# All transfers of the softmax sums in the order in which they become ready, in GpSimd's and SyncE's queues

## The chip, the cores and the metric

The kernel runs on one core of a Trainium2 chip. The metric is the device time of one execution in microseconds. Five engines work side by side, each through its own list of instructions in a fixed order: TensorE (PE), VectorE (DVE), ScalarE (ACT), GpSimd (POOL) and SyncE (SP). The last two mostly issue DMA transfers here. An instruction whose semaphores are not yet set holds everything behind it on the same engine.

## The reference

Two layers on x of shape (16, 256, 32, 32). Each adds to x a self-attention of its group-normalised input, with 4 heads of 64 channels over the 1024 positions:

```python
q, k, v = (einsum('oc,bcn->bon', W, xf) + b for each of q, k, v)     # 4 heads of d = 64
sim  = einsum('bhdi,bhdj->bhij', q, k)
qpos = einsum('hdi,bhdj->bhij', (rel_h + rel_w), q)
attn = softmax(sim + qpos, axis=-1)
out  = einsum('bhdn,bhmn->bhdm', v, attn)
x = x + out
```

The softmax needs, for each of 1024 query positions of each head, the sum of 1024 exponentials. How these sums are brought together is what the change touches.

## The kernel before

The schedule is written out by hand; nothing reorders it. A *unit* is one image in one layer, 32 in all. A unit has four *blocks*: two pairs of heads (`pr`) by two halves of the query positions (`half`), 128 blocks n = 0 to 127. An *even* block has half 0, an *odd* one half 1; the two blocks of one pair of heads are A (even) and B (odd) below. In tile names the numbers are unit, pair and half: `acc_21_0_1` belongs to unit 21, pair 0, half 1, which is block 85.

In a block TensorE makes eight score tiles (L539) on banks that DVE has seeded with the position term (L503), ACT takes the exponential of each into a tile `p` (L552), TensorE multiplies by the values (L592) and ACT copies the output out (L653, once a block, at its end). The projections of a later unit are woven in between.

The eight `p` of a block, each 128 key positions by 2 heads by 512 queries, are added up in these steps, which the page names by line:

- L557, DVE: `first` = p0 + p1, and `acc` = p3 + p4; L572, DVE: p5, p6, p7 are added to `acc`. The addition of p7 stands in the next block: at its start if that block is even, near its middle if it is odd.
- L568, POOL: a DMA of 512 KB that adds p2 to `first`. It is issued with `add_up(blk, 1)`.
- L609, POOL (`add_first`): 512 KB, adds `first` to `acc`; it needs the addition of p7.
- L614, POOL (`fold`): 256 KB, adds the upper 64 partitions of `acc` to the lower 64.
- L628, SP (`stack_up`): two of 64 KB, copy 32 partitions of `acc` into rows of `stack`, which A and B share.
- L633, POOL (`fold_again`): two of 64 KB, add the other 32 partitions of `acc` to the same rows. With them `acc` is free.
- L638, POOL (`fold_stack`): five transfers that halve the stack's 128 rows to 4, called D (64 rows onto 64, 128 KB), R (32), R/2 (16), R/4 (8) and R/8 (4 rows, 8 KB) after their argument. Each needs the one before it.
- L646, SP (`spread_sums`): four of 2 KB, bring the four rows into `den_all`.
- L688, DVE, and L690, L695, SP (`reciprocals`): 1/sum, sent to DRAM and from there back to all partitions in two copies of 256 KB. In an odd block this stands right behind the addition of A's p7.

Each POOL and SP transfer waits, at its place in the queue, until the ones that it depends on have landed. `first` and `acc` come from one pool of four buffers. Loads of x (L113) and stores of the output (L712) are in SP's queue too.

Of the kernel before, what the change touches and what calls it, by code (L numbers as in the profile page):

```python
# [56 lines left out]
def fast_path(ctx, tc, sh, x, layers, out, W, den_all, good, flag):  # L57
# [27 lines left out]
    B, C, H, N, CC, NT, NH, D, GT = (  # L85
        sh.B, sh.C, sh.H, sh.N, sh.CC, sh.NT, sh.NH, sh.D, sh.GT
    )
# [520 lines left out]
    def add_first(blk):  # L608
        nc.gpsimd.dma_start(accs[blk], firsts.pop(blk), accum_op=ALU.add)  # L609
# [25 lines left out]
    def fold_stack(u, pr, rows_):  # L635

        stack = stacks[u, pr]
        nc.gpsimd.dma_start(stack[:rows_], stack[rows_ : 2 * rows_], accum_op=ALU.add)  # L638

    def spread_sums(u, pr):  # L640

        stack, n = stacks.pop((u, pr)), index[u, pr, 0]
        for x in range(2):
            for h, hs in enumerate(QUARTERS):
                g = 2 * x + h
                nc.sync.dma_start(den_all[hs, n + x, :], stack[g : g + 1, :])  # L646
# [141 lines left out]
    def block(n):  # L788
# [11 lines left out]
        summed = blocks[n - 4][:2] if even and n > 3 else None  # L800
# [10 lines left out]
        if folded and even:  # L811
            add_first(previous)
        if even:
# [17 lines left out]
            if summed:  # L831
                fold_stack(*summed, R // 8)
                spread_sums(*summed)
# [38 lines left out]
            if folded:  # L872
                fold_again(previous)
            norms(u, b, 2)
# [26 lines left out]
            if summed and n == FOLDED:  # L901
                reciprocals(*summed)
# [5 lines left out]
        else:  # L908
# [11 lines left out]
            if stacked:  # L920
                fold_stack(*stacked, D)
            if stacked:
                fold_stack(*stacked, R)
            if not plain:
                k_half(w, pr, 1, qk)
# [15 lines left out]
            if folded:  # L941
                add_first(previous)
            if n > 4 and not last:
                reciprocals(*blocks[n - 5][:2])
# [20 lines left out]
            scores(after, 0)  # L965
            if folded:
                fold(previous)
                stack_up(previous)
            if stacked:
                fold_stack(*stacked, R // 2)  # L970
            if folded:
                fold_again(previous)
# [5 lines left out]
            if stacked:  # L978
                fold_stack(*stacked, R // 4)
                if last:  # L980
                    fold_stack(*stacked, R // 8)
                    spread_sums(*stacked)
# [528 lines left out]
```

## Time and profile before

| | us |
|---|---|
| median of 3 runs | 2529.62 |
| lowest, highest | 2519.19, 2544.5 |
| profiled execution | 2537.24 |
| its span, first to last instruction | 2535.5 |
| busy: PE, DVE, ACT, POOL | 2482.9, 2362.9, 2057.3, 796.4 |

The granted TensorE clock of the profiled execution was 0.995 of full speed. Busy times overlap, since the engines run side by side; POOL's busy time is that of issuing its transfers, most of its time it waits. In a row of the timeline stand the start, the duration, the engine, the line and the tiles (written <- read), and in brackets how long the engine was idle before it and what ended that. A transfer's own time is not its row's duration but the time to its landing, which the DMA view gives as a median for each kind.

### The profile page before, as it was taken

The numbers are of one execution on the slowest core, as the hardware profiler recorded it, in microseconds if no ns is written. First come the engines' busy times: TensorE is split into PE (matmuls) and PEld (weight loads), VectorE is DVE, ScalarE is ACT, GpSimd is POOL, SyncE is SP. The second block draws the span as 40 slices with busy tenths as digits, with TensorE's granted clock in tenths as the row PEclk, the third lists the DMA queues.
The fourth block names the chain that finished last, engine by engine and source line by source line (L and its number), as shares of the span: only waits on it lengthen the run. The fifth ranks groups of instructions, "written<-read, shape, count | busy, mean of one in ns | idle before, by whom it ended". The sixth has DMA issues, their size and how long they took to land. (4 is left out here: it accounts for less than half of the span.)

```text
span 2535.5 us, 86433 instructions
## 1 busy us (share of the span) xinstructions
PE 2482.9 (98%) x36976; PEld 1766.0 (70%) x36976; DVE 2362.9 (93%) x2816; ACT 2057.3 (81%) x4296; POOL 796.4 (31%) x937
## 2 busy tenths in 40 slices
PE   7999999999999999999999999999999999999997
PEld 4777777777767767777676777767776676677764
DVE  7899999999999999899999999999999999899998
ACT  5888888888888888788887888888878888788764
POOL 0223333333333333333332333333333333333230
PEclk9999999999999999999999999999999999999999
DMA  2555556566556555665565556565665555556552
GB/s 86 111 96 104 109 111 112 110 129 137 111 109 141 112 105 111 124 120 113 116 115 118 114 111 121 108 132 115 120 126 119 114 104 112 109 95 122 113 112 73
DMA packets 137704, 286.64 MB, mean 113 GB/s; under 512 B 55896, under 2 KB 57432, under 8 KB 137312
## 3 DMA queue, kind: packets, MB, share of 16 engines
q0 software_dynamic: 71568, 195.12, 44.6%
q1 hardware_dynamic: 65744, 85.90, 11.9%
q8 instruction: 293, 4.80, 0.8%
q14 instruction: 99, 0.81, 0.1%
HBM read 51.78 MB, written 17.30 MB: 27 GB/s over the span
## 5 line engine op out<-in xcount | busy, mean ns | idle before, releaser
L503 DVE TENSOR_TENSOR banks<-abt 128x1024 f32<-128x1024 f32 x1207 | 1239.6, 1060 | 100.5 <-ACT p L552 58.6
L552 ACT ACTIVATE p<-banks,shift 128x1024 f32<-128x1024 f32 x898 | 980.1, 1114 | 278.1 <-PE banks L539 162.4
L539 PE MATMUL banks<-q,k 64*64 64x512 f32 x8192 | 1114.5, 593 | 9.6 <-DVE banks L503 9.6
L592 PE MATMUL banks<-p,v 64*64 64x256 f32 x16384 | 963.6, 377 | 0.0
L592 PEld LDWEIGHTS banks<-p,v 64*64 64x64 f32 x16384 | 783.1, 133 | 182.6 <-issue 38.9
L539 PEld LDWEIGHTS banks<-q,k 64*64 64x64 f32 x8192 | 470.9, 133 | 305.6 <-issue 121.4
L633 POOL DMA_DIRECT2D stack<-acc x248 | 210.8, 964 | 842.2 <-DMA stack<-acc 688.1
L572 DVE TENSOR_TENSOR acc<-acc,p 128x1024 f32<-128x1024 f32 x372 | 454.0, 1220 | 4.2
L638 POOL DMA_DIRECT2D stack<-stack x310 | 309.9, 1000 | 386.4 <-DMA stack<-stack 225.1
L401 PE MATMUL banks<-t,form 64*64 64x512 f32 x1984 | 405.2, 589 | 0.0
L437 PE MATMUL banks<-Wv,xn 64*64 64x256 f32 x4096 | 302.1, 378 | 0.7 <-ACT v L462 0.7
L437 PEld LDWEIGHTS banks<-Wv,xn 64*64 64x64 f32 x4096 | 229.8, 133 | 43.6 <-PEq L193 17.5
L401 PE MATMUL banks<-xn,form 64*64 64x512 f32 x992 | 259.3, 589 | 0.0
L288 ACT ACTIVATE xn<-x,nshift,rstd 128x128 f32<-128x128 f32 x496 | 211.7, 500 | 29.4 <-DVE nshift L281 29.4
L568 POOL DMA_DIRECT2D first<-p x124 | 220.6, 1779 | 36.7 <-ACT p L552 33.3
L614 POOL DMA_DIRECT2D acc<-acc x124 | 103.1, 831 | 386.0 <-DMA acc<-first 373.4
L213 ACT ACTIVATE junk<-x,neg 128x128 f32<-128x128 f32 x505 | 199.9, 404 | 0.0
L609 POOL DMA_DIRECT2D acc<-first x124 | 185.5, 1496 | 36.6 <-DVE acc L572 33.3
L401 PEld LDWEIGHTS banks<-t,form 64*64 64x64 f32 x1984 | 137.7, 133 | 71.1 <-issue 33.9
L557 DVE TENSOR_TENSOR acc<-p,p 128x1024 f32<-128x1024 f32 x128 | 156.2, 1221 | 32.0 <-issue 18.2
L550 ACT ACTIVATE p<-banks,shift 128x512 f32<-128x512 f32 x252 | 159.5, 684 | 23.1 <-PE banks L539 17.3
L557 DVE TENSOR_TENSOR first<-p,p 128x1024 f32<-128x1024 f32 x124 | 150.9, 1217 | 2.4 <-DMA acc<-first 2.1
(102 smaller groups left out, 1761.9 us busy)
## 6 DMA issues: line engine op xcount, KB each, us to landing
first<-p POOLq DMA_DIRECT2D x124, 512.0 KB, 8.0
acc<-first POOLq DMA_DIRECT2D x124, 512.0 KB, 5.6
rden<-rd SPq DMA_DIRECT2D x126, 256.0 KB, 4.4
acc<-acc POOLq DMA_DIRECT2D x124, 256.0 KB, 4.5
x<-in_x_dram SPq DMA_DIRECT2D x32, 512.0 KB, 3.8
stack<-acc SPq DMA_DIRECT2D x248, 64.0 KB, 2.1
stack<-acc POOLq DMA_DIRECT2D x248, 64.0 KB, 2.8
out_dram<-x SPq DMA_DIRECT2D x31, 512.0 KB, 2.9
```

What stands on the lines that cost most here:

```text
L288: nc.scalar.activation(grouped(xns[u], g), grouped(xt[units[u][0]], g), AF.Identity, bias=shift[:, g : g + 1], scale=rstd[:, g : g + 1],)
L401: yield nc.tensor.matmul(ps[c, a, :], f[rs, left[a], c0 : c0 + D], right[a][rs, :], start=(t == 0 and step == 1 and a == 1), stop=(t == 1) ...
L437: yield nc.tensor.matmul(pv[c, a, i, :], xns[u][rs, cc, j0 : j0 + D], W.wv[l][rs, cc, :], start=(t == 0 and cc == 0 and i == 0), stop=(t = ...
L503: nc.vector.tensor_tensor(ps[:, h].rearrange("p h (w y) -> p h w y", y=H), ab[:, h, :H].unsqueeze(2).to_broadcast(shape), ab[:, h, H + hal ...
L539: nc.tensor.matmul(ps[c, h, :], a[hs, j0 : j0 + D], b[hs, columns], start=bool(tag) and i == 0, stop=i == len(terms) - 1, skip_group_check ...
L552: nc.scalar.activation(p, ps, AF.Exp, bias=W.shift)
L557: nc.vector.tensor_tensor(t, probs[blk, a], probs[blk, b], ALU.add)
L568: nc.gpsimd.dma_start(firsts[blk], probs[blk, 2], accum_op=ALU.add)
L572: nc.vector.tensor_tensor(accs[blk], accs[blk], probs[blk, j], ALU.add)
L592: yield nc.tensor.matmul(po[c, a, :QUART], vts[u, j // 4][rs, j % 4, c0 : c0 + D], p[rs, h, a * QUART : (a + 1) * QUART], start=(fresh and ...
L633: nc.gpsimd.dma_start(at, acc[R:D, h, :], accum_op=ALU.add)
L638: nc.gpsimd.dma_start(stack[:rows_], stack[rows_ : 2 * rows_], accum_op=ALU.add)
```

## The change

The steps and their sizes stay. Their places in the block's code move: A's `fold_again` and D go into the even block after the pair, R/2, R/4, R/8 and the spreads into the odd block after it, `stack_up` of A behind the spreads.

```diff
--- before.py
+++ after.py
@@ -797,7 +797,6 @@
             return block_without_pieces(n, half)
 
         stacked = blocks[n - 3][:2] if not even and n > 2 else None
-        summed = blocks[n - 4][:2] if even and n > 3 else None
         before = blocks[n - 6][:2] if even and n > 5 else blocks[n - 5][:2] if last else None
         after, previous = blocks[n + 1], blocks[n - 1] if n > 0 else None
         two = u + 2 < NU
@@ -810,6 +809,8 @@
             add_up(previous, 7)
         if folded and even:
             add_first(previous)
+            if n > 1:
+                fold_again(blocks[n - 2])
         if even:
             qk = psum2(tz, f"qk_{w}_{pr}") if not plain else None
             first = None if plain else first_product(w, pr, qk)
@@ -828,9 +829,6 @@
                 after_first(w, pr, qk)
             scores(blk, 2)
             add_up(blk, 1)
-            if summed:
-                fold_stack(*summed, R // 8)
-                spread_sums(*summed)
             v(1)
             if folded:
                 fold(previous)
@@ -871,6 +869,8 @@
             seed(after, 0, ta)
             if folded:
                 fold_again(previous)
+                if n > 1:
+                    fold_stack(*blocks[n - 2][:2], D)
             norms(u, b, 2)
             values_of_p = attend(blk, po, fresh=False)
             values_of_p(0)
@@ -898,8 +898,8 @@
             scores(after, 1)
             seed(after, 2, ta)
             add_up(blk, 6)
-            if summed and n == FOLDED:
-                reciprocals(*summed)
+            if n == FOLDED:
+                reciprocals(*blocks[n - 4][:2])
             seed(after, 3, tb)
             norms(u, b, 4)
             values_of_p(1)
@@ -918,9 +918,8 @@
                 reduced(2, 1)
                 added(2)
             if stacked:
-                fold_stack(*stacked, D)
-            if stacked:
                 fold_stack(*stacked, R)
+                fold_stack(*stacked, R // 2)
             if not plain:
                 k_half(w, pr, 1, qk)
             norms(u, b, 0)
@@ -940,6 +939,8 @@
             add_up(previous, 7)
             if folded:
                 add_first(previous)
+            if stacked:
+                fold_stack(*stacked, R // 4)
             if n > 4 and not last:
                 reciprocals(*blocks[n - 5][:2])
             scores(blk, 6)
@@ -963,23 +964,19 @@
             if two:
                 mean_out = (norm_mean if b == 1 else norm_var)(u + 2, pm)
             scores(after, 0)
+            if stacked:
+                fold_stack(*stacked, R // 8)
             if folded:
                 fold(previous)
-                stack_up(previous)
-            if stacked:
-                fold_stack(*stacked, R // 2)
-            if folded:
-                fold_again(previous)
             if u + 3 < NU and units[u + 3][1] == 0 and u > 0 or n == 3:
                 load_x(units[u + 3][0], range(pr_, pr_ + 1) if u > 0 else range(CC))
             seed(after, 1, tx)
             if last:
                 finish(*before)
             if stacked:
-                fold_stack(*stacked, R // 4)
-                if last:
-                    fold_stack(*stacked, R // 8)
-                    spread_sums(*stacked)
+                spread_sums(*stacked)
+            if folded:
+                stack_up(previous)
             if two:
                 mean_out()
                 if b == 3:
```

The POOL queue of before, from the L609 of block 84 (unit 21, pair 0, half 0) on; `stack_20_1` is the stack of the pair before it:

```order
L609 DMA acc_21_0_0_20257<-first_21_0_0_20107 128x1024
L568 DMA first_21_0_1_20383<-p_21_0_1_2_20329 128x1024
L614 DMA acc_21_0_0_20257<-acc_21_0_0_20257 64x1024
L638 DMA stack_20_1_19997<-stack_20_1_19997 16x512
L633 DMA stack_21_0_20477<-acc_21_0_0_20257 32x512 x2
L638 DMA stack_20_1_19997<-stack_20_1_19997 8x512
L609 DMA acc_21_0_1_20426<-first_21_0_1_20383 128x1024
L568 DMA first_21_1_0_20580<-p_21_1_0_2_20578 128x1024
L638 DMA stack_20_1_19997<-stack_20_1_19997 4x512
L614 DMA acc_21_0_1_20426<-acc_21_0_1_20426 64x1024
L633 DMA stack_21_0_20477<-acc_21_0_1_20426 32x512 x2
L638 DMA stack_21_0_20477<-stack_21_0_20477 64x512
```

and now:

```order
L609 DMA acc_21_0_0_20258<-first_21_0_0_20112 128x1024
L638 DMA stack_20_1_20006<-stack_20_1_20006 8x512
L568 DMA first_21_0_1_20385<-p_21_0_1_2_20330 128x1024
L638 DMA stack_20_1_20006<-stack_20_1_20006 4x512
L614 DMA acc_21_0_0_20258<-acc_21_0_0_20258 64x1024
L609 DMA acc_21_0_1_20428<-first_21_0_1_20385 128x1024
L633 DMA stack_21_0_20487<-acc_21_0_0_20258 32x512 x2
L568 DMA first_21_1_0_20585<-p_21_1_0_2_20583 128x1024
L614 DMA acc_21_0_1_20428<-acc_21_0_1_20428 64x1024
L633 DMA stack_21_0_20487<-acc_21_0_1_20428 32x512 x2
L638 DMA stack_21_0_20487<-stack_21_0_20487 64x512
L638 DMA stack_21_0_20487<-stack_21_0_20487 32x512
```

B's L609 (`acc_21_0_1`) stood behind A's `fold_again` (L633) and stands ahead of it; R/2, R/4 and R/8 of the older stack stood behind L614, L633 and L568, and stand ahead of L609, L568 and L614; R/2 follows R at once.

SP's queue of before at the same place, from the reciprocals of unit 20, pair 0 on:

```order
L690 DMA rd_20_0_20371<-r8_20_0_20369 128x16
L695 DMA rden_20_0_20373<-rd_20_0_20371 64x1024 x2
L628 DMA stack_21_0_20477<-acc_21_0_0_20257 32x512 x2
L113 DMA x_13_20483<-in_x_dram 128x1024
L646 DMA den_all_58<-stack_20_1_19997 64x1x8 x4
L628 DMA stack_21_0_20477<-acc_21_0_1_20426 32x512 x2
L690 DMA rd_20_1_20834<-r8_20_1_20832 128x16
L695 DMA rden_20_1_20836<-rd_20_1_20834 64x1024 x2
```

and now:

```order
L690 DMA rd_20_0_20373<-r8_20_0_20371 128x16
L695 DMA rden_20_0_20375<-rd_20_0_20373 64x1024 x2
L113 DMA x_13_20480<-in_x_dram 128x1024
L646 DMA den_all_58<-stack_20_1_20006 64x1x8 x4
L628 DMA stack_21_0_20487<-acc_21_0_0_20258 32x512 x2
L628 DMA stack_21_0_20487<-acc_21_0_1_20428 32x512 x2
L690 DMA rd_20_1_20836<-r8_20_1_20834 128x16
L695 DMA rden_20_1_20838<-rd_20_1_20836 64x1024 x2
```

The spreads (L646) stood ahead of B's `stack_up` and stand ahead of A's.

The DVE's list keeps its order, but the pool gives out its four buffers in another rotation, since they are given back at other places. What the L557 of blocks 84 to 86 wait for, before (DMASW are semaphores of POOL's transfers, DMAHW of SP's):

```order
L557 TENSOR_TENSOR first_21_0_0_20107<-p_21_0_0_0_19994,p_21_0_0_1_20073 128x1024 [waits DMASW6_49,DMASW5_49]
L557 TENSOR_TENSOR acc_21_0_0_20257<-p_21_0_0_3_20139,p_21_0_0_4_20155 128x1024 [waits DMAHW2_49,DMASW7_49,DMAHW3_49,DMASW2_49,DMASW1_49]
L557 TENSOR_TENSOR first_21_0_1_20383<-p_21_0_1_0_20244,p_21_0_1_1_20264 128x1024 [waits DMASW6_49,DMASW4_49]
L557 TENSOR_TENSOR acc_21_0_1_20426<-p_21_0_1_3_20339,p_21_0_1_4_20347 128x1024 [waits DMAHW1_49,DMASW7_49,DMAHW2_49,DMASW1_49,DMASW0_49]
L557 TENSOR_TENSOR first_21_1_0_20580<-p_21_1_0_0_20474,p_21_1_0_1_20538 128x1024 [waits DMASW5_49,DMASW4_49]
```

and now:

```order
L557 TENSOR_TENSOR first_21_0_0_20112<-p_21_0_0_0_19996,p_21_0_0_1_20078 128x1024 [waits DMASW7_49,DMASW6_49]
L557 TENSOR_TENSOR acc_21_0_0_20258<-p_21_0_0_3_20139,p_21_0_0_4_20155 128x1024 [waits DMASW3_49,DMASW0_49]
L557 TENSOR_TENSOR first_21_0_1_20385<-p_21_0_1_0_20245,p_21_0_1_1_20265 128x1024 [waits DMAHW0_49,DMASW5_49,DMAHW7_49,DMASW4_49,DMASW2_49]
L557 TENSOR_TENSOR acc_21_0_1_20428<-p_21_0_1_3_20340,p_21_0_1_4_20348 128x1024 [waits DMAHW1_49,DMASW7_49,DMAHW2_49,DMASW1_49,DMASW0_49]
L557 TENSOR_TENSOR first_21_1_0_20585<-p_21_1_0_0_20476,p_21_1_0_1_20543 128x1024 [waits DMASW6_49,DMASW5_49]
```

An even `acc` waited for `stack_up` and `fold_again` of the A before it, and now waits for the L609 of the block before it, whose `first` held the buffer. An odd `first` waited for the L609 of two blocks before, and now waits for `stack_up` and `fold_again` of the A of the pair before. An even `first` (L609 of two blocks before) and an odd `acc` (`fold_again` of two blocks before) wait as they did.

## The prediction

> **What bounds the kernel now.** I read the page first, for who is busy, then equal stretches of work side by side, then who the VectorE waits for, then the two DMA queues in order of time.
>
> ```profile
> span 2535.5 us, 86433 instructions
> PE 2482.9 (98%) x36976; PEld 1766.0 (70%) x36976; DVE 2362.9 (93%) x2816; ACT 2057.3 (81%) x4296; POOL 796.4 (31%) x937
> ```
>
> By the page TensorE sets the time. But a unit of work (four blocks; the counts differ by records that are missing) does not always take equally long. The view of stretches, with PE, weight loads, DVE, ACT and POOL busy in that order, then the granted clock, shows two units:
>
> ```profile
> 190.70:267.20 76.50, 76.50 (x1160) 54.95 (x1154) 73.00 (x88) 64.79 (x140) 25.22 (x30) 1.00 0.55 103
> 1310.30:1389.90 79.60, 76.82 (x1156) 54.96 (x1152) 73.25 (x88) 64.81 (x138) 25.65 (x31) 1.00 0.58 114
> ```
>
> 76.50 us is the undisturbed unit, where PE never idles; the second took 3.1 us more at the same clock and the same DVE work. How much that comes to over the run follows from the first and last copy of an output (L653, once a block) of 30 whole units, blocks 4 to 123:
>
> ```profile
> 114.17 0.57 ACT L653 COPY od<-banks 128x512 f32<-128x512 f32 x1
> 2442.14 0.59 ACT L653 COPY od<-banks 128x512 f32<-128x512 f32 x1 [2.33 <-PE banks L592]
> ```
>
> 2442.1 - 114.2 = 2327.9 us; 30 x 76.50 = 2295.0. So **32.9 us** are lost. Who loses them is in the view of L557, the DVE additions that open a new buffer `first` or `acc`: before them the DVE sat idle until
>
> ```profile
>   issue: 18.2, 20
>   DMA stack<-acc: 13.2, 8
>   DMA acc<-first: 2.5, 3
> ```
>
> 33.9 us in 31 waits (the "issue" ones have no releaser in the records, but stand at the same place, before `acc`). The two sums agree to 1 us: the lost time is DVE waiting for a buffer that the GpSimd queue has not yet freed. DVE then seeds the score banks late and PE stands. The queue itself waits almost always, and for what is in the view of waits:
>
> ```profile
> POOL stack L633 <- DMA stack<-acc: 688.1, 105, 9.7
> POOL acc L614 <- DMA acc<-first: 373.4, 121, 6.2
> POOL acc L609 <- DVE acc L572: 33.3, 2, 30.5
> ```
>
> It waits for its own earlier transfers, and only twice in 124 blocks for the DVE to hand it a new sum (L609), both in the first blocks. So it never catches up: it runs at its own pace. That pace is in the row of L609 in the view of the tile `acc`:
>
> ```profile
> L609 POOL DMA_DIRECT2D acc<-first x124: 870/1205/1906, 65.4 to 2455.2; - x124
> ```
>
> (2455.2 - 65.4) / 123 x 2 = 38.86 us a pair of blocks, where the undisturbed pair is 76.50 / 2 = 38.25. 0.61 us too much over 60 pairs is 36 us, near the 32.9 lost. **The kernel is paced by a serial chain of transfers that is 1.6% slower than TensorE.**
>
> **One turn of the chain.** The queue in order of time, from the L609 of block 84 to that of block 86 (start, duration, what; in brackets the idle time before), and below it SyncE's part:
>
> ```profile
> 1696.64 1.20 POOL L609 DMA_DIRECT2D acc<-first  x1
> 1703.57 0.82 POOL L614 DMA_DIRECT2D acc<-acc  x1 [4.82 <-DMA acc<-first]
> 1710.22 1.69 POOL L633 DMA_DIRECT2D stack<-acc  x2 [5.03 <-DMA stack<-acc]
> 1711.82 1.87 POOL L609 DMA_DIRECT2D acc<-first  x1
> 1717.80 0.84 POOL L614 DMA_DIRECT2D acc<-acc  x1 [1.86 <-DMA acc<-first]
> 1726.87 1.71 POOL L633 DMA_DIRECT2D stack<-acc  x2 [8.23 <-DMA stack<-acc]
> 1730.63 0.82 POOL L638 DMA_DIRECT2D stack<-stack  x1 [2.05 <-DMA stack<-acc]
> 1734.94 0.78 POOL L638 DMA_DIRECT2D stack<-stack  x1 [3.49 <-DMA stack<-stack]
> 1735.45 1.20 POOL L609 DMA_DIRECT2D acc<-first  x1
> ```
>
> ```profile
> 1707.68 1.13 SPq L628 DMA_DIRECT2D stack<-acc  x2
> 1721.79 2.42 SPq L646 DMA_DIRECT2D den_all<-stack  x4
> 1724.32 1.17 SPq L628 DMA_DIRECT2D stack<-acc  x2
> ```
>
> Call the even block A and the odd one B. Link by link: add A's `first` 6.93, fold A until SyncE stacks it 4.11, stacking 2.54, second fold into the stack 1.60, add B's `first` 5.98, fold B 6.52 (2.5 of it SyncE's four spreads, which stand ahead of the stacking), stacking 2.55, until D (the 64-row fold of the stack) 3.76, until R (32 rows) 4.31, until the next L609 0.51: 38.81 us.
>
> **The change part by part.** No transfer is added or removed, and PE, DVE and ACT keep their order. Landing times from the DMA view:
>
> ```profile
> first<-p POOLq DMA_DIRECT2D x124, 512.0 KB, 8.0
> acc<-first POOLq DMA_DIRECT2D x124, 512.0 KB, 5.6
> stack<-acc POOLq DMA_DIRECT2D x248, 64.0 KB, 2.8
> stack<-stack POOLq DMA_DIRECT2D x62, 64.0 KB, 2.5
> stack<-stack POOLq DMA_DIRECT2D x62, 8.0 KB, 6.5
> ```
>
> (the 8 KB fold lands late because it stands behind the 512 KB of L568). For L609 with L568 about 2 us behind it, as the new order has it, there are rows of the first blocks, when the queue still kept up:
>
> ```profile
> 98.71 0.84 POOL L638 DMA_DIRECT2D stack<-stack  x1 [2.95 <-DMA stack<-acc]
> 101.66 0.79 POOL L638 DMA_DIRECT2D stack<-stack  x1 [2.11 <-DMA stack<-stack]
> 105.23 0.89 POOL L609 DMA_DIRECT2D acc<-first  x1 [2.78 <-DVE acc L572]
> 107.30 0.86 POOL L568 DMA_DIRECT2D first<-p  x1 [1.18 <-DVE first L557]
> 111.66 0.82 POOL L614 DMA_DIRECT2D acc<-acc  x1 [3.49 <-DMA acc<-first]
> ```
>
> The new turn, us from A's L609:
>
> - R/4 (8 rows) needs R/2, issued 0.5 earlier: 2.2. L568 behind it: 2.7. R/8 needs R/4: about 6. A's fold L614: 6.43 by the early rows and 0.5 for the issue of R/8: 6.9. B's L609 is next in the queue: 7.4 at the earliest. Now it no longer waits for A to be stacked; this is the wait that goes, some 6 us of the old turn.
> - On SyncE the spreads come ahead of A's stacking. R/8 lands behind L568, 2.7 + 8.0 = 10.7; four spreads 2.5: 13.2; stacking 2.55: A's second fold L633 at 15.8. L568 of the next block 16.9, B's fold 17.8 (B's L609, 5.6, landed by then).
> - B's fold lands behind that L568 (16.9 + 5.6, nothing large ahead of it) and its own 1.5 (half of the 3.0 by which L568 lands after an L609 issued 0.6 before it): 24.0. No spreads ahead of the stacking now, so 2.5 us go here: 24.1; L633 26.7; D after 3.76: 30.4; R after 2.95 as in the early rows (at that time SyncE's two 256 KB copies don't run beside it): 33.4; then R/2, which now waits for R, after 2.7: 36.1; L609 0.5: **36.6 us**, 2.2 less than the old turn and 1.6 less than the 38.25 that TensorE gives it.
>
> The Trainium skill (DMA: Bandwidth & Descriptors, Anatomy of one DMA) gives a GpSimd-issued transfer 2.0 us fixed plus bytes / 436e3, which speaks against small dependent folds in a row: each pays it. By it the landings of D and R in the path cost 2.3 + 2.15 = 4.45 us by estimate; the rows above give 2.95 + 2.7 = 5.65, so the turn would be 35.4 by the page. The measured landings decide, and the verdict would be the same.
>
> Both ends: 34.2 us if the L568 ahead of R/8 lands in 5.6 instead of 8.0, and 39.6 if R and R/2 each take the 4.31 that the quoted turn shows from D to R. I take 36.6, near the early rows: the 4.31 was taken while SyncE's two 256 KB copies (L695) ran, and those start only after a reciprocal that follows A's last addition, while R now goes some 5 us ahead of that addition.
>
> One cost stands in no row above: A's stacking is now issued while B's L609 may be in flight. What SyncE's small transfers can suffer is in the landings of the spreads (L646):
>
> ```profile
> DMA to landing us min/median/max: 1.7/1.8/3.7
> ```
>
> The slowest takes twice the usual time. The bounds for A's stacking are then: no delay, and held until B's L609 has landed. The same page (Queues, rings and completion order) says that a semaphore's increment lands only after every earlier write of that DMA engine, across its queues; by that rule it would be the upper bound. When B's L609 goes depends on the DVE:
>
> ```profile
> 1106.24 1.22 DVE L572 TENSOR_TENSOR acc<-acc,p 128x1024 f32<-128x1024 f32 x1
> 1117.33 2.48 DVE L572 TENSOR_TENSOR acc<-acc,p 128x1024 f32<-128x1024 f32 x2
> 1120.86 1.22 DVE L557 TENSOR_TENSOR first<-p,p 128x1024 f32<-128x1024 f32 x1
> 1132.06 1.22 DVE L557 TENSOR_TENSOR acc<-p,p 128x1024 f32<-128x1024 f32 x1
> ```
>
> A's sum is ready at 1107.5, B's at 1119.8, 12.3 later. So if the queue has caught up, B's L609 goes at 12.3, lands at 17.9, and A's L633 moves from 15.8 to at most 18.1: the turn then takes up to 38.9. But a queue that is late issues B's L609 sooner, down to 7.4, and the delay goes: its own pace is 36.6. It settles a few us behind the DVE and stays there.
>
> How late may it be? In the new order an even `acc` takes the buffer that B's L609 frees: 1119.8 + 5.6 = 1125.4 against a need at 1132.1, 6.7 to spare. An even `first` needs A's L609: 1107.5 + 6.4 against 1120.9, 7.0 to spare. Odd blocks take buffers that the second folds free; B's, the later one, has landed at 26.7 + 0.6 + 2.8 = 30.1, and the need comes after the next A's sum, at 38.25. So lateness under 6 us costs nothing, and 1.6 us a turn are made up.
>
> **Sum.** All waits of the 30 units go: 2537.24 (the profiled execution, 1.7 above its span) - 32.9 = 2504.3. I leave 0.7 us for a stray wait: **2505 us**. What is late next is nothing: the unit is at 76.50, which the first units show with PE busy throughout. The profiled execution stands 7.6 above the median 2529.62, which by this reading had some 25 us of the same waits; the floor is common, so the gain on the median is 25 us, 1.0%. About 1% is also what a measurement of this kernel can tell from no change.
>
> **The rivals.**
>
> - The queue stays a little too slow: one of R and R/2 meets SyncE's copies, a load of x or a store (+1.4), and A's stacking is held by 0.5 on the mean: 38.5. For it: 4.31 in the quoted turn. Against: R's new place. 0.25 x 60 = 15 us stay: 2520.
> - **Slower:** the folds that now stand in a row. In the old order R/2, R/4 and R/8 are issued beside other waits; in the new one L609 stands behind R and R/2 both. If each takes 4.31, the turn is 39.6, and 1.35 x 60 = 81 us come over the floor: 2585. It decides from 38.86 a turn on, the old pace. Against: 2.95 and 2.5 in the rows without copies beside them.
> - The change does not do what it says: the waits move from `acc` to `first` or to the reciprocal, whose sums come by the same chain, and the total stays: 2530. Against: 6.7 and 7.0 us to spare at the new places, and the spreads now come earlier.
>
> **How the numbers follow.** Forecast (2500 to 2511) 0.67; queue a little too slow (2511 to 2531) 0.18; slower (2531 to 2600) 0.09; unchanged (2525 to 2535) 0.06. Range 2499 to 2527: the forecast and most of the second case, 0.81. Faster by over 1% means under 2504.3, the floor itself and what the last blocks may add to it: 0.42. Slower by over 1%, above 2555: 0.06. Within: 0.52.
>
> **What would show it.** L609 waiting for DVE L572 in most blocks instead of twice; L557 idle under 3 us in all; units of 76.50 throughout; A's L633 15 to 18 us after its L609; R and R/2 about 2.7 us apart. I am wrong if L609 still never waits for the DVE, or if units of 76.50 show up while the total does not fall.

## The result and the profile after

The changed kernel is slower: 2660.7 us in the median (2651.31 to 2662.86), against 2531.45 us for the kernel before beside it (2519.19 to 2544.5). The ratio is 1.050, with an interval of 1.044 to 1.056. The forecast was 2505 us.

The page of the changed kernel, the span and the busy times:

```profile
span 2658.2 us, 86471 instructions
PE 2536.6 (95%) x36976; PEld 1758.5 (66%) x36976; DVE 2356.5 (89%) x2816; ACT 2056.2 (77%) x4296; POOL 792.6 (30%) x937
```

DVE, ACT and POOL do the same work as before, within 1%; PE's share fell from 98% to 95%, and DVE's from 93% to 89%. So there is more waiting, not more work. (TensorE ran the same 36976 instructions too; why its busy time is 54 us longer stays open.) What L557 waited for, where 33.9 us stood before:

```profile
  DMA acc<-first: 97.6, 48
  issue: 15.6, 15
  DMA stack<-stack: 7.2, 3
  DMA stack<-acc: 3.3, 2
```

123.7 us, and most of it at another place: an even `first`, whose buffer A's L609 frees. The view of waits has two more lines to read:

```profile
ACT p L552 <- DMA first<-p: 107.2, 40, 4.4
POOL acc L609 <- DVE acc L572: 46.1, 6, 30.5
```

The first is new (0.8 us before): ACT waits to write a `p` buffer that L568 has not yet read. The second is the sign that the prediction asked for, L609 waiting for DVE "in most blocks": it did so 6 times. So the sign of being wrong came, "if L609 still never waits for the DVE", but for 6 of 124 blocks. The queue is later than before. Its pace, from the row of L609 in the view of the tile `acc`:

```profile
L609 POOL DMA_DIRECT2D acc<-first x124: 870/902/1213, 65.6 to 2574.0; - x124
```

(2574.0 - 65.6) / 123 x 2 = 40.79 us a pair of blocks, where 36.6 were forecast, 38.86 stood before, and TensorE gives 38.25. The excess over TensorE, 2.54 x 61.5 = 156 us, is the loss: 2660 - 156 = 2504, the floor of the prediction. Two stretches show when it begins, the first a unit and the second 80 us of the later run (length, then PE, weight loads, DVE, ACT, POOL busy, the granted clock):

```profile
190.70:267.20 76.50, 76.50 (x1156) 54.95 (x1152) 72.98 (x88) 64.82 (x139) 24.04 (x29) 1.00 0.54 99
1500.00:1580.00 80.00, 77.43 (x1142) 54.30 (x1138) 71.84 (x87) 64.01 (x137) 23.85 (x29) 1.00 0.53 102
```

The first is undisturbed; in the later 80 us PE is busy for 77.43, at the same clock. From the first to the last copy of an output of the 30 whole units (L653), a unit takes 81.64 us here and 77.60 before.

**One turn of the changed chain.** The GpSimd queue from the L609 of block 108 to that of block 110, then SyncE's part:

```profile
2279.75 1.18 POOL L609 DMA_DIRECT2D acc<-first  x1
2281.77 0.81 POOL L638 DMA_DIRECT2D stack<-stack  x1 [0.85 <-DMA stack<-stack]
2282.30 1.21 POOL L568 DMA_DIRECT2D first<-p  x1
2285.44 0.81 POOL L638 DMA_DIRECT2D stack<-stack  x1 [1.94 <-DMA stack<-stack]
2285.97 1.16 POOL L614 DMA_DIRECT2D acc<-acc  x1
2288.61 0.90 POOL L609 DMA_DIRECT2D acc<-first  x1 [1.48 <-DVE banks L503]
2296.65 1.68 POOL L633 DMA_DIRECT2D stack<-acc  x2 [7.15 <-DMA stack<-acc]
2297.72 1.51 POOL L568 DMA_DIRECT2D first<-p  x1
2298.26 1.83 POOL L614 DMA_DIRECT2D acc<-acc  x1
2308.54 1.69 POOL L633 DMA_DIRECT2D stack<-acc  x2 [8.45 <-DMA stack<-acc]
2312.63 0.84 POOL L638 DMA_DIRECT2D stack<-stack  x1 [2.39 <-DMA stack<-acc]
2317.75 0.79 POOL L638 DMA_DIRECT2D stack<-stack  x1 [4.29 <-DMA stack<-stack]
2320.48 0.77 POOL L638 DMA_DIRECT2D stack<-stack  x1 [1.94 <-DMA stack<-stack]
2321.01 1.18 POOL L609 DMA_DIRECT2D acc<-first  x1
```

```profile
2289.74 3.21 SPq L646 DMA_DIRECT2D den_all<-stack  x4
2293.06 2.24 SPq L628 DMA_DIRECT2D stack<-acc  x2
```

```profile
2306.00 1.11 SPq L628 DMA_DIRECT2D stack<-acc  x2
2310.10 0.33 SPq L690 DMA_DIRECT2D rd<-r  x1
2312.37 1.11 SPq L695 DMA_DIRECT2D rden<-rd  x2
```

Three places cost more than forecast. B's fold is issued at 2298.26 and B's stacking at 2306.00, 7.74 us later, with the 512 KB of L568 issued 0.54 ahead of the fold. D is issued at 2312.63, 0.26 us after SyncE's copies of `rden` (L695), and R follows only after 5.12 us. R itself has no copy beside it, and R/2 follows after 2.73, as forecast. And A's stacking, at 2293.06, releases A's L633 after 3.59 us instead of 2.55, with B's L609 (2288.61) ahead of it. The row of B's L609 names L503 of DVE, but what it waited for is L568 (2282.30), which had landed 0.56 us before it; in all of the 51 turns below B's L609 goes 0.55 to 0.83 us after that landing.

That this is the rule shows in the mean over 51 turns (A is block 18 to 118), worked out from the issue times in the traces, us after A's L609. "Stack" is SyncE's L628; the three folds of the stack are those of this pair:

| kernel | L614 A | L609 B | stack A | L633 A | L614 B | stack B | L633 B | D | R | R/2 | next L609 |
|---|---|---|---|---|---|---|---|---|---|---|---|
| forecast | 6.9 | 7.4 | 13.2 | 15.8 | 17.8 | 24.1 | 26.7 | 30.4 | 33.4 | 36.1 | 36.6 |
| after | 7.05 | 9.19 | 12.89 | 16.60 | 18.36 | 25.44 | 28.07 | 32.54 | 36.65 | 40.45 | 41.03 |
| before | 6.08 | 14.89 | 10.41 | 13.19 | 20.89 | 26.99 | 29.73 | 34.10 | 38.28 | – | 38.86 |
| sum_first_alone | 6.27 | 9.59 | 10.70 | 15.35 | 20.76 | 26.68 | 29.52 | 33.77 | 37.65 | – | 38.23 |
| spreads_behind_a_stacking | 6.94 | 9.44 | 11.15 | 15.46 | 17.20 | 24.15 | 26.85 | 31.12 | 34.68 | 38.65 | 39.23 |
| fold_again_back | 7.17 | 15.90 | 11.95 | 14.71 | 21.73 | 26.31 | 29.00 | 33.47 | 37.94 | 41.33 | 41.91 |
| spreads_behind_b_stacking | 6.59 | 16.41 | 11.61 | 14.66 | 22.56 | 27.16 | 29.89 | 34.39 | 37.67 | – | 38.32 |
| r2_behind_l609 | 6.12 | 14.03 | 13.01 | 15.87 | 19.66 | 26.25 | 29.09 | 33.31 | 36.40 | 39.66 | 38.27 |
| b_fold_ahead_of_l568 | 7.29 | 9.74 | 13.67 | 17.05 | 18.21 | 22.77 | 26.82 | 30.90 | 34.25 | 37.96 | 38.54 |
| reciprocals_9us_later | 7.29 | 9.63 | 13.38 | 17.04 | 18.85 | 25.76 | 28.40 | 32.78 | 36.12 | 40.37 | 40.95 |
| copies_behind_a_stacking | 7.23 | 10.86 | 13.18 | 17.30 | 19.44 | 26.26 | 28.96 | 33.46 | 36.55 | 39.44 | 40.53 |

("–": R/2 stands in the next turn there. A turn near 38.25 is TensorE's pace, at which the queue has time left.)

Up to B's fold the forecast is met within 1 us, but for B's L609, and A's L633 leads straight to B's fold (1.76 us instead of 7.70). The error grows from there on.

### The profile page after: what moved, and what is told of

It is laid out like the page before. It is cut to its first block, busy times and chain, and to the rows that moved or that the text cites. A ratio compares the mean times of both kernels' runs of the same rounds, so it can differ in the third digit from the quotient of the medians.

```text
span 2658.2 us, 86471 instructions
## 1 busy us (share of the span) xinstructions
PE 2536.6 (95%) x36976; PEld 1758.5 (66%) x36976; DVE 2356.5 (89%) x2816; ACT 2056.2 (77%) x4296; POOL 792.6 (30%) x937
## 3 DMA queue, kind: packets, MB, share of 16 engines
HBM read 51.78 MB, written 17.30 MB: 26 GB/s over the span
## 4 chain that ended last, share of the span: by engine, by line
DMA 54%; issue 17%; PE 9%; POOL 9%; SPq 5%; DVE 5%; ACT 1%; POOLq 0%; DVEq 0%; ACTq 0%
DMA stack<-stack 19%; DMA acc<-acc 18%; DMA stack<-acc 15%; SPq L646 4%; POOL stack L638 4%; PE banks L539 4%; POOL stack L633 3%; PE banks L592 3%; DVE banks L503 2%; POOL acc L609 2%; SPq L628 1%; DMA first<-p 1%; PE banks L401 1%; PE banks L437 1%; DVE acc L565 1%
## 5 line engine op out<-in xcount | busy, mean ns | idle before, releaser
L503 DVE TENSOR_TENSOR banks<-abt 128x1024 f32<-128x1024 f32 x1207 | 1234.7, 1058 | 141.5 <-ACT p L552 101.5
L539 PE MATMUL banks<-q,k 64*64 64x512 f32 x8192 | 1133.5, 598 | 84.6 <-DVE banks L503 84.5
L592 PEld LDWEIGHTS banks<-p,v 64*64 64x64 f32 x16384 | 801.6, 133 | 162.3 <-issue 35.7
L539 PEld LDWEIGHTS banks<-q,k 64*64 64x64 f32 x8192 | 440.7, 133 | 462.7 <-DVE banks L503 306.1
L638 POOL DMA_DIRECT2D stack<-stack x310 | 250.1, 807 | 774.9 <-DMA stack<-stack 580.5
L633 POOL DMA_DIRECT2D stack<-acc x248 | 209.3, 954 | 891.2 <-DMA stack<-acc 792.7
L401 PE MATMUL banks<-t,form 64*64 64x512 f32 x1984 | 412.1, 591 | 0.0
L401 PE MATMUL banks<-xn,form 64*64 64x512 f32 x992 | 281.2, 593 | 0.0
L557 DVE TENSOR_TENSOR first<-p,p 128x1024 f32<-128x1024 f32 x124 | 151.1, 1218 | 102.9 <-DMA acc<-first 95.4
L401 PEld LDWEIGHTS banks<-t,form 64*64 64x64 f32 x1984 | 149.1, 133 | 79.1 <-issue 43.4
L614 POOL DMA_DIRECT2D acc<-acc x124 | 178.0, 1436 | 4.8 <-DMA acc<-first 3.3
L557 DVE TENSOR_TENSOR acc<-p,p 128x1024 f32<-128x1024 f32 x128 | 155.9, 1218 | 21.2 <-issue 15.6
L568 POOL DMA_DIRECT2D first<-p x124 | 163.4, 1318 | 36.3 <-ACT p L552 32.7
L550 ACT ACTIVATE p<-banks,shift 128x512 f32<-128x512 f32 x252 | 158.9, 682 | 17.5 <-PE banks L539 16.6
L609 POOL DMA_DIRECT2D acc<-first x124 | 127.7, 1030 | 107.3 <-DVE acc L572 46.1
```

Source lines behind the costliest of these rows:

```text
L401: yield nc.tensor.matmul(ps[c, a, :], f[rs, left[a], c0 : c0 + D], right[a][rs, :], start=(t == 0 and step == 1 and a == 1), stop=(t == 1) ...
L503: nc.vector.tensor_tensor(ps[:, h].rearrange("p h (w y) -> p h w y", y=H), ab[:, h, :H].unsqueeze(2).to_broadcast(shape), ab[:, h, H + hal ...
L539: nc.tensor.matmul(ps[c, h, :], a[hs, j0 : j0 + D], b[hs, columns], start=bool(tag) and i == 0, stop=i == len(terms) - 1, skip_group_check ...
L557: nc.vector.tensor_tensor(t, probs[blk, a], probs[blk, b], ALU.add)
L592: yield nc.tensor.matmul(po[c, a, :QUART], vts[u, j // 4][rs, j % 4, c0 : c0 + D], p[rs, h, a * QUART : (a + 1) * QUART], start=(fresh and ...
L633: nc.gpsimd.dma_start(at, acc[R:D, h, :], accum_op=ALU.add)
```

## The experiments

The ratios are to the kernel before, run beside each on the same chip. Its median there was 2525 to 2540 us, so a difference between two rows of this table is good to some 10 us.

| kernel | made from | median us | ratio, interval |
|---|---|---|---|
| spreads_behind_b_stacking | before | 2506.63 | 0.987, 0.983 to 0.990 |
| sum_first_alone | before | 2504.67 | 0.987, 0.982 to 0.992 |
| sum_first_and_spreads | before | 2504.92 | 0.991, 0.989 to 0.993 |
| fold_again_back | after | 2726.78 | 1.075, 1.070 to 1.079 |
| spreads_behind_a_stacking | after | 2552.01 | 1.005, 1.002 to 1.008 |
| b_fold_ahead_of_l568 | after | 2530.70 | 1.003, 1.001 to 1.005 |
| both_mends | after | 2503.66 | 0.987, 0.984 to 0.989 |
| r2_behind_l609 | spreads_behind_a_stacking | 2502.84 | 0.991, 0.988 to 0.993 |
| reciprocals_late | after | 2816.51 | 1.113, 1.109 to 1.117 |
| reciprocals_9us_later | after | 2669.96 | 1.053, 1.049 to 1.057 |
| copies_behind_a_stacking | after | 2645.23 | 1.047, 1.044 to 1.051 |

### Does the queue pace the kernel before? The spreads behind B's stacking

```diff
                 fold_stack(*summed, R // 8)
-                spread_sums(*summed)
             v(1)
...
                 stack_up(previous)
+            if summed:
+                spread_sums(*summed)
             scores(blk, 5)
```

> The kernel before with SyncE's four spreads (L646) moved from ahead of B's stacking (L628) to behind it; the GpSimd queue is not touched. If the serial chain of the queue paces the kernel before, as the prediction read it, the 2.5 us of the spreads leave the turn: 38.9 - 2.5 = 36.4 us, under TensorE's 38.25, and the time is that of the undisturbed units, 2500 to 2512 us, with VectorE's wait at L557 under 5 us in all. If something else paces it (the lost time is not this queue's), it stays at 2525 to 2540 us.

2506.63 us. The row of L609 and all that L557 waited for:

```profile
L609 POOL DMA_DIRECT2D acc<-first x124: 870/1200/1908, 65.8 to 2420.7; - x124
```

```profile
  ACT p L552: 0.3, 1
```

38.29 us a pair, and L557 no longer waits for any transfer. Four 2 KB transfers moved on SyncE took 1.3% off the time; PE, DVE, ACT and the GpSimd queue have the same instructions in the same order. The reading of the kernel before, a chain of transfers that is 0.6 us a pair too slow, is shown, and with it a floor near 2505.

### Which part of the change is to blame? Three undone or done alone

One part done alone, B's L609 ahead of A's `fold_again` (R/4, which stood behind it, moves too):

```diff
             add_first(previous)
+            if n > 1:
+                fold_again(blocks[n - 2])
+        if summed:
+            fold_stack(*summed, R // 4)
         if even:
...
-            if folded:
-                fold_again(previous)
...
             if stacked:
-                fold_stack(*stacked, R // 4)
                 if last:
+                    fold_stack(*stacked, R // 4)
                     fold_stack(*stacked, R // 8)
```

> The kernel before with one part of the change alone: B's L609 is issued ahead of A's fold_again (L633), and R/4 with it; R/2, R/8, the spreads and the stacking stay where they were. Theory ROW (the change lost its time where the folds R, R/2 and R/4 each wait for the landing of the one before it ahead of the next 512 KB transfer): those folds are not moved here, so nothing is lost; L609 of A at 38 to 39 us a turn, 2505 to 2535 us. Theory HOLD (B's L609, in flight early, holds A's stacking on SyncE until it has landed, and that is what made the changed kernel slow): the same hold is here, A's L633 moves from 13.2 to 15 or later, and the time is 2560 us or more.

The same move of `fold_again` undone in the changed kernel (R/4 stays):

```diff
             add_first(previous)
-            if n > 1:
-                fold_again(blocks[n - 2])
...
                 stack_up(previous)
+                fold_again(previous)
```

> The changed kernel with A's fold_again (L633) back ahead of B's L609, so that B's L609 cannot be in flight while A is stacked; R, R/2 and R/4 stay in a row ahead of L609 and L568, the spreads stay ahead of A's stacking. Theory HOLD: the cause is gone, A's stacking to L633 takes 2.55 us again, and the time falls to that of the kernel before, 2530 us, or below. Theory ROW: D, R and R/2 still cost 3.8 us more a turn than before, and B's fold is later by some 4 us as in the kernel before: a turn of 41 us or more, 2650 to 2800 us.

2504.67 and 2726.78 us. Both come out on ROW's side: the part alone reaches the floor, and without it the changed kernel gets worse. HOLD as the cause of the slowdown falls. That the folds in a row cost time is not shown by these two; it is tested below. The hold itself is real, and the table shows it: from A's stacking to A's L633 pass 2.8 us before, 2.8 in fold_again_back and 2.9 in r2_behind_l609, where B's L609 goes later than the stacking; where it goes earlier, they are 3.7 after, 4.3 in spreads_behind_a_stacking and 4.7 in sum_first_alone. It costs 1 to 2 us where the prediction expected it to vanish, but B's earlier fold is worth more.

The spreads put back behind A's stacking:

```diff
-            if stacked:
-                spread_sums(*stacked)
             if folded:
                 stack_up(previous)
+            if stacked:
+                spread_sums(*stacked)
```

> The changed kernel with SyncE's spreads (L646) put back behind A's stacking (L628); nothing else is moved. Theory SPREADS (A's stacking waits for the spreads, whose R/8 lands late): A's stacking goes at about 11 us instead of 12.9, A's L633 up to 1.6 us earlier, the turn 39.4 instead of 41.0 and the time about 2570 us. Theory HOLD: the stacking is issued earlier but lands no sooner, since B's L609 is in flight: within 0.5 us a turn, 2630 to 2665 us. Theory ROW says little of this part: at most the 1.6 us, and the time stays over 2560 us.

2552.01 us, a turn of 39.23: 1.80 less, a little more than SPREADS expected, since 1.14 us come at A's L633 and the later folds meet less as well. So the change took the spreads out of B's path and put them into A's. They are worth about 109 us, and yet the kernel stays slower than before by 0.5%: they are not the whole cause.

### R/2 ahead of L609

```diff
                 fold_stack(*stacked, R)
-                fold_stack(*stacked, R // 2)
...
             if stacked:
-                fold_stack(*stacked, R // 4)
+                fold_stack(*stacked, R // 2)
...
-            if stacked:
-                fold_stack(*stacked, R // 8)
             if folded:
                 fold(previous)
+            if stacked:
+                fold_stack(*stacked, R // 4)
+                fold_stack(*stacked, R // 8)
```

> The kernel spreads_behind_a_stacking (2552 us, a turn of 39.2) with R/2 moved from ahead of A's L609 to right behind it, and R/4 and R/8 from ahead of L568 and of A's fold (L614) to behind A's fold. Theory ROW: the wait of R/2 for R's landing, 3.97 us from R to R/2 in that kernel's mean turn, leaves the path, and R/4 and R/8 cost about 0.5 more ahead of B's L609: 39.2 - 3.4 = 35.8, under 38.25, so 2503 to 2515 us. Rival: R and R/2 only fill time in which the turn waits for something else (B's chain or VectorE): the turn stays near 39 and the time within 10 us of 2552.

2502.84 us, ROW's figure. D, R, L609 and R/2 of one turn:

```profile
2090.39 0.82 POOL L638 DMA_DIRECT2D stack<-stack  x1 [2.91 <-DMA stack<-acc]
2093.38 0.79 POOL L638 DMA_DIRECT2D stack<-stack  x1 [2.16 <-DMA stack<-stack]
2095.07 0.91 POOL L609 DMA_DIRECT2D acc<-first  x1 [0.91 <-DVE r L688]
2096.14 0.80 POOL L638 DMA_DIRECT2D stack<-stack  x1 [0.16 <-issue]
```

L609 goes 1.69 us after R and is released by DVE, not by a fold (the row names L688, which stands right behind the addition of p7): the queue waits for the sum again, and in 41 of 51 turns A's L609 goes within 0.6 us of the end of that addition. Three edits in one, so the 49 us are not R/2's alone; but the fold that stood ahead of L609 is gone, and with it the wait.

### B's fold behind L568

```diff
             scores(blk, 2)
-            add_up(blk, 1)
-            v(1)
             if folded:
                 fold(previous)
+            add_up(blk, 1)
+            v(1)
```

> The changed kernel with B's fold (L614) issued ahead of the next block's L568 instead of 0.6 us behind it. Theory BEHIND (B's fold lands only when the 512 KB of that L568 have landed, so B's stacking comes 7.1 us after the fold's issue): B's stacking comes 4.0 to 5.0 us after it, some 2.5 us a turn go, and the time is 2500 to 2540 us. Rival: the fold takes 7 us by itself at this place: within 15 us of 2661.

2530.70 us; B's fold to B's stacking takes 4.56 us in the mean instead of 7.08. One turn, GpSimd's queue and SyncE's:

```profile
1326.64 1.48 POOL L614 DMA_DIRECT2D acc<-acc  x1
1327.26 1.79 POOL L568 DMA_DIRECT2D first<-p  x1
```

```profile
1331.93 1.12 SPq L628 DMA_DIRECT2D stack<-acc  x2
```

BEHIND is shown: issued 0.6 us behind the 512 KB of L568 on the same queue, the 256 KB fold takes 7.04 us to land in the mean, 1.8 us after L568; issued 0.6 us ahead, it takes 4.53, and L568 lands 3.1 us after it. These 2.5 us a turn bring the time back to that of the kernel before. In the old order L568 stood 5.40 us ahead of B's fold instead of 0.56; the change brought the two together, because it took away the wait between them.

### Both mends

The two edits above, the spreads behind A's stacking and B's fold ahead of L568, together in the changed kernel.

> The changed kernel with the two edits that each helped: the spreads behind A's stacking (2552 us, turn 39.2) and B's fold ahead of the next L568 (2531 us, turn 38.5); B's L609 ahead of A's fold_again and R and R/2 in a row ahead of A's L609 stay as changed. If the two costs are separate links of one chain they add: 41.0 - 1.8 - 2.5 = 36.7 us a turn, under TensorE's 38.25, so 2502 to 2510 us with L557 waiting under 5 us. If they were one cost (both free the same wait), the turn stays at 38.3 to 38.6 and the time at 2515 to 2535 us.

2503.66 us, so they are not one cost: together they bring the kernel to the floor, which neither does alone. That they add up to 4.3 us a turn can't be read off, because the turn (38.28) stops at TensorE's pace. All of L557's waits are

```profile
  DMA acc<-first: 1.9, 1
  ACT p L552: 0.3, 1
```

So the changed order is not bad as such: B's L609 first, R and R/2 in a row ahead of L609 are kept here, and the kernel is 1.3% faster than the one before.

### Why R came 4.1 us after D, and R/2 3.8 us after R: the copies of `rden`

The reciprocals, behind which SyncE sends the copies, moved behind A's stacking in the same block:

```diff
-            if n > 4 and not last:
-                reciprocals(*blocks[n - 5][:2])
...
                 stack_up(previous)
+            if n > 4 and not last:
+                reciprocals(*blocks[n - 5][:2])
```

> The changed kernel with the reciprocals (L688, L690, L695), which stand behind A's last addition in the odd block, moved behind A's stacking in the same block, so that SyncE's two 256 KB copies no longer run beside D, R and R/2. Theory COLLISION (those copies are why D, R and R/2 took 4.5, 4.1 and 3.8 us to the next step and not the 3.8, 2.95 and 2.7 of the prediction): these three come back to within 0.3 us of the predicted ones, some 2.5 us a turn, and, if the copies cost nothing at their new place, the time is about 2661 - 57 x 2.5 = 2520 us; where they slow B's fold by 1 us, 2575 us. Rival: the three folds are as slow without the copies (their landings are set by something else): the steps stay over 4.0, 4.0 and 3.6 us and the time at 2640 us or more.

```profile
DVE od L703 <- DMA rden<-rd: 283.5, 60, 7.6
```

2816.51 us: the copies came too late, and DVE waited 283.5 us to multiply by them, which says nothing of the folds. The folds themselves:

```profile
1317.46 0.84 POOL L638 DMA_DIRECT2D stack<-stack  x1 [2.31 <-DMA stack<-acc]
1320.46 0.78 POOL L638 DMA_DIRECT2D stack<-stack  x1 [2.16 <-DMA stack<-stack]
1323.21 0.77 POOL L638 DMA_DIRECT2D stack<-stack  x1 [1.97 <-DMA stack<-stack]
```

3.00 from D to R and 2.75 from R to R/2, the forecast's numbers; in the mean of 51 turns 3.22 and 2.78. The third step that COLLISION named did not come back: from B's L633 to D pass 4.51 us in the mean, as in the changed kernel (4.47). What is slow there is L633, and not for the copies. A smaller move of the same two lines, behind `add_up(blk, 4)`:

> The changed kernel with the reciprocals moved about 9 us later, behind the DVE additions of p2 to p4 in the same odd block. (Behind A's stacking they were so late that the multiplication by them, L703, waited 7.6 us for rden in every pair, so that kernel's time, 2816 us, says nothing of the folds; but R and R/2 there took 3.2 and 2.8 us to the next step, not 4.1 and 3.8.) Theory COLLISION: R and R/2 take 3.0 to 3.4 and 2.7 to 3.1 us here too, L703 waits under 1 us a pair, the turn falls by 1.5 to 2 us and the time to 2545 to 2580 us; if the copies now slow A's fold by 1 us, up to 2615. Rival: R and R/2 were quick there only because the queue was not late; then they stay over 3.9 and 3.6 here and the time within 15 us of 2661.

2669.96 us, no gain, and the edit did not do what its label says: the copies moved only from 8.2 to 4.7 us ahead of the next L609 in the mean. There they met R and R/2 instead of D: from D to R pass 3.34 us in the mean, from R to R/2 4.25, so neither theory's numbers came. One turn, GpSimd's queue and the copies:

```profile
1325.81 0.84 POOL L638 DMA_DIRECT2D stack<-stack  x1 [2.37 <-DMA stack<-acc]
1328.80 0.78 POOL L638 DMA_DIRECT2D stack<-stack  x1 [2.15 <-DMA stack<-stack]
1334.85 0.77 POOL L638 DMA_DIRECT2D stack<-stack  x1 [5.26 <-DMA stack<-stack]
```

```profile
1328.79 1.11 SPq L695 DMA_DIRECT2D rden<-rd  x2
```

Here R went 0.01 us after the copies and took 6.05 us to the next step, where D, free of them, took 2.99; a load of x, issued at 1329.96, was in flight too. The landing times of the 51 turns, sorted by whether copies of `rden`, and loads of x or stores besides, were in flight (mean us; number of transfers):

| kernel, fold | copies alone | copies and a load or store | neither |
|---|---|---|---|
| after, D | 3.80 (31) | 3.87 (19) | 2.67 (1) |
| after, R | 3.26 (18) | 4.25 (19) | 2.84 (11) |
| after, R/2 | – | 4.10 (1) | 2.29 (49) |
| reciprocals_9us_later, D | 2.69 (2) | – | 3.05 (49) |
| reciprocals_9us_later, R | 3.74 (31) | 4.25 (20) | – |
| reciprocals_9us_later, R/2 | 2.83 (27) | 3.43 (20) | 2.27 (3) |
| copies_behind_a_stacking, D | – | – | 2.79 (51) |
| copies_behind_a_stacking, R | – | – | 2.59 (51) |
| copies_behind_a_stacking, R/2 | – | – | 2.88 (51) |

(The five beside a load or store alone are left out. In the last kernel, where many landings of loads and stores are missing, all 51 are counted and loads and stores aren't told apart; no fold there is beside a copy.) The slow landing goes with the copies, from fold to fold, and R is slowest where a load or a store runs beside it as well. The Trainium skill (DMA: Bandwidth & Descriptors, Issuing engines are not separate DMA queues) says that transfers issued by SyncE and GpSimd run on the same 16 DMA engines and interleave; these rows agree.

Last, the copies alone moved, with the reciprocals left on DVE where they are:

```diff
-                reciprocals(*blocks[n - 5][:2])
+                reciprocals(*blocks[n - 5][:2], held=True)    # without the two copies
...
                 stack_up(previous)
+            if n > 4 and not last:
+                copies(*blocks[n - 5][:2])
```

> The changed kernel with the reciprocals where they are on VectorE and their store (L690) too, but SyncE's two 256 KB copies back (rden) issued behind A's stacking, where GpSimd's queue has B's fold and the next L568 and none of D, R and R/2. Theory COLLISION: D, R and R/2 land without the copies in 2.7 to 3.0, 2.5 and 2.3 us, the steps from D to R and from R to R/2 fall from 4.1 and 3.8 to 3.2 and 2.8, and the turn by these 1.9 us unless the copies slow B's fold: 2661 - 57 x 1.9 = 2553 us, 2610 us where B's fold takes 1 us more; L703 waits for rden under 1 us a pair. Rival: the steps get shorter but the copies cost as much at the new place, so the time stays within 20 us of 2661: then the collision is a price of the transfers and not of their place.

(In this kernel L703 is line 712.) 2645.23 us: against the changed kernel nothing that can be told apart. The steps did fall, to 3.09 and 2.89 us (from B's L633 to D it stayed at 4.50), and L557's 123.7 us of waits went to

```profile
  ACT p L552: 0.3, 1
```

but another wait took their place:

```profile
DVE od L712 <- DMA rden<-rd: 134.6, 58, 5.6
```

134.6 us are about what the kernel still loses over the floor (2645 - 2504 = 141). So the COLLISION is shown for the landings, but its price in time is not: the time is where the rival put it, within 20 us of 2661, because the cost turned into a wait that neither theory had in its sum. What the queue's own pace would be without the copies stays open, since it had 40.5 us for each turn here.

### Is there more below the floor? The two edits to the kernel before together

> The kernel before with the two edits that each brought it to about 2505 us, together: B's L609 and R/4 ahead of A's fold_again, and the spreads behind B's stacking. If the undisturbed units of 76.50 us are a floor set by TensorE, it cannot go below it: 2502 to 2507 us, no more than 2 us under either alone, though the queue now has more to spare. If the queue still costs either of them something, it falls by more than 2 us below both, under 2502 us.

2504.92 us, 1.7 us under the one (2506.63) and 0.3 over the other (2504.67), as expected of a floor. Five orders of these transfers end between 2502.8 and 2506.6 us, and a unit takes 76.50 to 76.61 us in them, measured over 30 units: with the queue out of the way, the undisturbed unit remains. Any of the five beats both kernels; spreads_behind_b_stacking does it with one moved line.

## Why the prediction was wrong

**Right: what bounds the kernel, the floor, and the wait that goes.** spreads_behind_b_stacking showed the bound and the floor. B's L609 ahead of A's `fold_again` brought B's fold to 1.76 us behind A's L633, as the sum had it (2.0); alone, with R/4, it is worth 1.3%.

**Right as a rival, too small and too unlikely: the folds in a row.** The second rival gave 39.6 us a turn and 2585 us, deciding from 38.86. It was 41.03 and 2661. That it came near is in part luck: its two steps were cheaper than it said (4.11 and 3.80 us, not 4.31 each) and explain 2.3 us of the 4.4; the rest came from places that it does not name. The third rival named the place where the waits went, `first`, but with the total unchanged.

**Wrong: the sum of the turn, 36.6 instead of 41.03.** The 4.4 us by their terms:

- *D, R and R/2, 3.0 us; the step that failed.* Taken were 3.76 from B's L633 to D and then 2.95 and 2.7; measured 4.47, 4.11 and 3.80. The first 0.7 us are a price read from one turn: the quoted turn has 3.76, the mean of 51 turns of the kernel before 4.37. The copies are not its reason, since it is 4.51 and 4.50 in the two kernels that keep them away; what is stays open. The other 2.3 us go with the copies, and with the loads and stores beside them. Of the two prices in the trace, 2.95 and 4.31, I took the lower, since "R now goes some 5 us ahead of that addition"; that is the order of a queue that keeps up, and in the kernel before D to R took 4.18 in the mean.
- *B's fold behind L568, 0.8 us.* 6.3 us were taken from fold to stacking, measured 7.08. The larger fault is that the 2.5 us were there to be had and the prediction took them as given: it priced the fold "behind that L568" and never asked what it costs that L568 now stands right ahead of it.
- *The hold of A's stacking, 1.2 us, less 0.3.* "A queue that is late issues B's L609 sooner, down to 7.4, and the delay goes": it went at 9.19 in the mean, because it reads the `first` to which L568, issued at 2.60, still adds, which the prediction overlooked. It landed at 14.87 in the mean and was in flight in 50 of 51 turns when A's stacking went, at 12.89 in the mean.

With the forecast's three numbers for D, R and R/2 the mean turn would be 38.1, just under 38.25; with the share of the copies alone taken off, 38.8, the pace of the kernel before. So no single term explains the slowdown.

**Late or on time.** The copies follow DVE's clock and the folds the queue's; a queue that is 10 us late puts D and R right beside the copies. In r2_behind_l609 and both_mends, whose queues keep up, the copies go 1.6 us after and 0.3 us ahead of the next L609 in the mean, and from D to R pass 3.09 and 3.15 us. In the changed kernel they go 8.2 us ahead: in the 36 turns with 8 to 10 us, D to R/2 takes 8.0 us; in the three in which the copies go less than 4 us ahead or after, 6.5. The start of the run shows the slide: in the first nine turns the copies go at +1.3, -0.6, -3.5, -4.8, -9.4, -8.6, -9.5, -9.5 and -10.1 us from the next L609, and the turn is 38.3 in the first and 42.6 in the last of them. So being late makes these steps slower. But it did not start the slide. The second turn begins 0.3 us behind the end of A's last addition, on time, and takes 41.5; the third begins 3.7 behind it and takes 39.8. In them A's L633 goes at 17.9 and 17.3 (forecast 15.8), B's fold takes 6.7 and 6.6 us to its stacking (6.3), and 5.0 and 4.8 pass to D (3.76). The sum was too small for a queue on time as well.

**Wrong: what lateness costs.** "6.7 and 7.0 us to spare" was about right, and of no use against a queue that is 10 us late: in the mean A's L609 goes 10.4 us after the end of A's last addition, where it was 6.6 in the kernel before and 0.3 in the first turn. The 48 waits of L557 for an L609 are 2.0 us in the mean. That L568, late with the rest, would hold ACT's `p` was not foreseen.

Of the signs named in advance, A's L633 (15 to 18, measured 16.6) came; L609 waiting for DVE, L557 under 3 us, 76.50 throughout and R and R/2 2.7 us apart did not.

## What to carry to other kernels

Sorting a queue by when transfers become ready is no goal of its own: an order also decides which large transfer stands right ahead of a small one that someone waits for, and each small dependent fold ahead of the next large one is a landing in the path. When a serial chain paces a kernel by under 1 us a turn, move the cheapest link off it first (here four 2 KB transfers, past the one that was waited for). Take the prices of a new turn from the mean of many turns, not from one row each. And work it out for the lateness in which it would run, not only for a queue on time: two clocks that slide against each other can collide with what they missed.

## What the runs showed of the hardware

Here small transfers took longer to land beside large ones of the other queue. The four spreads, 1.8 us to land before, stand in the changed kernel at (least, median, most):

```profile
DMA to landing us min/median/max: 1.7/4.4/6.1
```

They are issued by SyncE, just after GpSimd has issued B's 512 KB. A's stacking shows how long such a transfer is held. In the changed kernel its first 64 KB took 3.12 us to land in the 50 turns with B's L609 in flight, and in all 50 they landed after B's L609, by 0.77 us in the median; in the one turn without, they took 1.99. In sum_first_alone they took 4.05 in 50 such turns and 1.98 in the one without; in 41 of the 50 they landed after B's L609, and in the median of all 50 by 0.19 us. The Trainium skill (DMA: Bandwidth & Descriptors, Queues, rings and completion order) says that an increment lands only after every earlier write of that DMA engine, across its queues. The 41 and 50 turns fit with it. The 9 others don't speak against it, since it is a rule for the writes of one engine and not for whole transfers, and which writes were the earlier ones was not looked at here. The upper bound that the prediction gave for this wait, held until B's L609 has landed, was thus nearly the usual case.
